# The first part of a convolution kernel with its TensorE work in blocks twice as long

## The chip, the cores and the metric

The kernel runs on one core of one Trainium2 chip. The metric is the device time of that core in microseconds (us). TensorE is called PE here, VectorE DVE, ScalarE ACT, GpSimd POOL, and SyncE SP, as in the profile.

## What is computed

The input x is 32 images of 128 channels of 64 x 64 pixels. The reference normalizes it in groups of four channels, and then convolves it through butterfly transforms along both image axes:

```python
def _kop2d(x, weight, kd1, kd2, k11, k12, k21, k22):
    x_f = tensor_product(xc, _c(k11), _c(k12), False)      # complex 64x64 matrices along h and w
    w_f = tensor_product(wc, _c(kd1), _c(kd2), False) * math.sqrt(H * W)
    prod = jnp.einsum('bihw,oihw->bohw', x_f, w_f)
    out = tensor_product(prod, _c(k21), _c(k22), True)
    return jnp.real(out)
...
x = x + _L0_conv_ref(_gn(x), ...)
t = _to_tokens(x)
t = t + _L1_attn_ref(_ln_t(t), ...)
t = t + _L1_ffn_ref(_ln_t(t), ...)                         # 8 experts, the best 2 weighted
```

## The kernel before

The kernel has three parts that follow each other. The first transforms the images (`x_f`) and writes the result to DRAM as `xf`. The second mixes the channels at every frequency. The third transforms back and does the attention and the experts. The change is in the first part alone.

In the first part, an image b goes through three kinds of PE work, each in pieces. A piece fills one PSUM tile, which another engine then copies out.

- `pz` (`turn_over`, line 373): 8 transposes of 128 x 128 turn a quarter of the image. Four pieces, g = 0 to 3. ACT copies each piece out into the tile `z` with four copies (`turned`, L383; planner keys `zo`, two copies each).
- `pv` (`along_w`, L396): 32 matmuls on 64 x 64 tiles of the array, the transform along W. Eight pieces. ACT copies each out into `v` with one copy (`w_out`, L407; key `vo`).
- `pf` (`along_h`, L418): 8 matmuls of 128 x 128, the transform along H. Eight pieces. The copy into a tile `f` (`h_out`, L428; key `fo`) is on DVE, but for every fourth piece (f3 and f7), where it is on ACT. Two DMAs on SP then write it to `xf` (`store`).

A float32 matmul that is not a transpose has two records in the trace: 64 pv records belong to one pv piece, 16 pf records to one pf piece.

All PSUM tiles of this part come from one pool with the tag "ps", four tiles of 4 KB per partition. The images, the tiles z, v and f come from pools of 3, 2, 2 and 4 buffers.

The work is pipelined over images in steps s = 0 to 33: in step s, PE does the pz pieces of image s, the pv pieces of image s-1 and the pf pieces of image s-2. The loop at the end of the part adds these pieces to a planner (`Plan`), with an estimated duration, a due time (`at`, in steps), what it comes after, and what it takes and frees ("ps" has room for 4). The order of the PE pieces is fixed: `add` chains each PE operation to the one added before. On every other engine the planner runs, of the operations that are ready by its estimates, the one that is due first. The instructions are then written out in the order that it found, and each engine runs its own in that order.

The group normalization of an image is spread over the step before its pz pieces. DVE takes eight statistics of 512 pixels (`bn_stats`, L319) as the loads of x land, and one aggregate (L328). Then a small PE matmul averages over the groups (L332, tile `gps`, which comes from the pool "ps" too), DVE computes the spread (L337 to L339), a second small matmul averages that (L342), DVE adds a constant (L345, after which `gps` is free), POOL takes the power (`grstd`, L349), and DVE scales the image in four pieces (L362). `norm_on_pe(b, 0)` adds the operations up to the first small matmul, `norm_on_pe(b, 1)` those from the second on. In the first four images the scaling is on ACT instead.

In the loop of before, a step has four equal blocks of one pz piece, two pv pieces and two pf pieces. The two small matmuls of the next image's normalization stand around the pz and pv pieces of one of these blocks:

```python
            for g in range(4):
                at = s + 0.25 * g
                if g == min(s, 3) - 1:
                    norm_on_pe(s + 1, 0)
                piece("pz", s, g, at)
                for k in range(2):
                    piece("pv", s - 1, 2 * g + k, at + 0.04 + 0.04 * k)
                if g == min(s, 3) - 1:
                    norm_on_pe(s + 1, 1)
```

Between steps 12 and 16, POOL prepares the convolution's weights, eight transposes on PE (`pwr`, L298, again a tile from "ps") turn them, and DVE copies them out (`wst`, L303).

Of the kernel before, what the change touches and what calls it, by code (L numbers as in the profile page):

```python
# [90 lines left out]
def kernel(  # L91
# [28 lines left out]
    pf = dram.tile([n, n, P * n], F32, name="pf")  # L120
# [42 lines left out]
    with ExitStack() as ph1:  # L163
# [12 lines left out]
        def add(key, engine, us, at, run, after=(), take=(), free=(), late=0.0):  # L176
            after = [made[k] for k in after if k in made]
            if engine == "PE":
                after += on_pe[-1:]
            made[key] = plan.add(engine, us, SLOT * at, run, after, take, free, late)  # L180
            if engine == "PE":
                on_pe.append(made[key])
# [184 lines left out]
        def turn_over(b, g):  # L367
            def run():
                ps = tile_of["pz", b, g] = pp.tile([P, 2, 512], F32, tag="ps", name=f"pz{b}_{g}")
                pv = ps.rearrange("w u (k c) -> w (u k) c", c=P)  # L370
                for k in range(8):
                    h = 2 * (8 * g + k)
                    nc.tensor.transpose(pv[:, k, :], xs[b][:, h * n : (h + 2) * n], ident)  # L373
            return run

        def turned(b, g, r):

            def run():
                if g == 0 and r == 0:
                    zs[b] = zp.tile([P, n, n], F32, tag="z", name=f"z{b}")  # L380
                pv = tile_of["pz", b, g].rearrange("w u (k c) -> w (u k) c", c=P)
                for half in range(2):
                    nc.scalar.copy(  # L383
                        zs[b][half * n : (half + 1) * n, :, 32 * r + 8 * g : 32 * r + 8 * g + 8],
                        pv[r * n : (r + 1) * n, :, half * n : (half + 1) * n].rearrange("w h c -> w c h"),
                    )
            return run

        def along_w(b, g):
            def run():  # L390
                ps = tile_of["pv", b, g] = pp.tile([P, 2, 512], F32, tag="ps", name=f"pv{b}_{g}")
                for k in range(8):
                    for half in range(2):
                        rows = slice(half * n, (half + 1) * n)
                        for r in range(2):
                            nc.tensor.matmul(  # L396
                                ps[r * n : (r + 1) * n, half, k * n : (k + 1) * n],
                                zs[b][rows, 8 * g + k, :], pw[rows, r, :], start=True, stop=True,
                            )
            return run  # L400

        def w_out(b, g):

            def run():
                if g == 0:
                    vs[b] = vp.tile([P, n, P], F32, tag="v", name=f"v{b}")
                nc.scalar.copy(  # L407
                    vs[b].rearrange("h w (a c) -> h w a c", a=2)[:, :, :, 8 * g : 8 * g + 8],
                    tile_of.pop(("pv", b, g)).rearrange("h a (c w) -> h w a c", w=n),
                )  # L410
            return run

        def along_h(b, g):
            def run():
                ps = tile_of["pf", b, g] = pp.tile([P, 2, 512], F32, tag="ps", name=f"pf{b}_{g}")
                pl = ps.rearrange("c u m -> c (u m)")
                for j in range(8):
                    nc.tensor.matmul(  # L418
                        pl[:, j * P : (j + 1) * P], vs[b][:, 8 * g + j, :], ph.rearrange("h r m -> h (r m)"),
                        start=True, stop=True,  # L420
                    )
            return run

        def h_out(b, g):
            def run():
                f = tile_of["f", b, g] = fp.tile([P, 8, 2 * n], F32, tag="f", name=f"f{b}_{g}")
                copy = nc.scalar.copy if g % 4 == 3 else nc.vector.tensor_copy
                copy(f.rearrange("c w m -> c (w m)"), tile_of.pop(("pf", b, g)).rearrange("c u m -> c (u m)"))  # L428
            return run

        def store(b, g):
            def run():
                f = tile_of.pop(("f", b, g))

                for k in range(0, 8, 4):
                    nc.sync.dma_start(xf[b, :, 8 * g + k : 8 * g + k + 4, :], f[:, k : k + 4])
            return run
# [52 lines left out]
        def piece(kind, b, g, at):  # L490
            if not 0 <= b < B:
                return
            if kind == "pz":
                add(
                    ("pz", b, g), "PE", 1.0, at, turn_over(b, g), [("nm", b, k) for k in range(4)],
                    ("ps",), ("x",) if g == 3 else (),
                )
                for r in range(2):
                    add(
                        ("zo", b, g, r), "ACT", 1.2, at, turned(b, g, r),  # L500
                        [("pz", b, g)] + [("pv", b - 2, k) for k in range(8)] + ([("zo", b, 0, 0)] if g or r else []),
                        (), ("ps",) if r else (),
                    )
            elif kind == "pv":
                add(
                    ("pv", b, g), "PE", 1.12, at, along_w(b, g),
                    [("zo", b, k, r) for k in range(4) for r in range(2)] + ["wi"], ("ps",),
                )
                add(
                    ("vo", b, g), "ACT", 1.02, at, w_out(b, g),  # L510
                    [("pv", b, g)] + [("pf", b - 2, k) for k in range(8)] + ([("vo", b, 0)] if g else []), (), ("ps",),
                )
            else:
                add(("pf", b, g), "PE", 1.95, at, along_h(b, g), [("vo", b, k) for k in range(8)], ("ps",))
                on_act = g % 4 == 3
                add(("fo", b, g), "ACT" if on_act else "DVE", 1.02 if on_act else 1.22, at, h_out(b, g), [("pf", b, g)], ("f",), ("ps",))
                add(("fs", b, g), "SP", 0.9, at, store(b, g), [("fo", b, g)], (), ("f",), 5.0)
# [7 lines left out]
        for s in range(B + 2):  # L525
            if s == 0:
                norm(2)
            for g in range(4):
                at = s + 0.25 * g
                if g == min(s, 3) - 1:  # L530
                    norm_on_pe(s + 1, 0)
                piece("pz", s, g, at)
                for k in range(2):
                    piece("pv", s - 1, 2 * g + k, at + 0.04 + 0.04 * k)
                if g == min(s, 3) - 1:
                    norm_on_pe(s + 1, 1)
                for k in range(2):
                    piece("pf", s - 2, 2 * g + k, at + 0.12 + 0.07 * k)
                    if 4 <= s + 2 < B:
                        piece_of_image(s + 2, 2 * g + k)  # L540
            if 3 <= s + 2 < B:
                norm(s + 2)
            if s == 0:
                norm_on_pe(1, 0)
                norm_on_pe(1, 1)
            if s == 3:
                butterfly(0, "POOL", nc.gpsimd, 3.2, 4.5)
                add("sel", "POOL", 2.5, 99, select, [("nm", 4, 3)])
            if s == 6:
                add("wr", "PE", 0.6, 6.0, weight_rows, [("b0", 5), "sel"], ("ps",))  # L550
                add("wd", "DVE", 0.8, 6.0, weight_matrices, ["wr"], (), ("ps",))
                butterfly(2, "POOL", nc.gpsimd, 7.0, 4.5)
                add("wo", "DVE", 1.2, 9.0, output_matrices, [("b2", 5)])
                add("wm", "SP", 0.5, 10.0, weight_taps, [("b2", 5)], (), (), 4.0)
            if 20 <= s < 24:
                add(("ew", s), "SP", 1.0, s, expert_load(s - 20), [("pf", s - 3, 4)], (), (), 4.0)
            if 12 <= s < 16:
                k = s - 12
                add(("wr", k), "POOL", 5.0, s - 0.5, onto_rows(k), ["wm", ("pf", s - 3, 4)], ("f",))
                add(("wt", k), "PE", 1.1, s, rows_turned(k), [("wr", k)], ("ps",))  # L560
                add(("we", k), "DVE", 1.25, s, rows_out(k), [("wt", k)], (), ("ps", "f"))
# [4 lines left out]
    with ExitStack() as ph2:  # L566
# [146 lines left out]
        for w in range(n):  # L713
# [9 lines left out]
            for half in range(2):  # L723
                for t in range(4):
                    at = w + 0.5 * half + 0.125 * t
# [718 lines left out]
```

## Time and profile before

| | |
|---|---|
| time, median of 3 runs | 6058.34 us (6054.57 to 6061.50) |
| the profiled execution: span | 6062.4 us, 4.1 above the median |
| TensorE clock, mean | 0.991 |
| PE busy | 5891.6 us, 97% |
| DVE, ACT, POOL busy | 4221.2, 3756.5, 4191.0 us |
| first pz to last pf of the first part | 21.3 to 931.0 us |
| pf matmuls, first part | 491.2 us in 4096 records |
| pv weight loads and matmuls | 16384 records each |
| xf stores | 512 DMAs of 256 KB, 3.3 us from issue to landing |
| x loads | 256 DMAs of 256 KB, 4.5 us from issue to landing |

The span goes from the first to the last instruction of the one execution that was profiled; the execution's own time is not in the list of runs, so its span is set beside them. Times of single instructions come from that execution. A row of a timeline gives the start in us, the length in us, the engine, the line, the operation, the tiles that it writes and reads, the shape and the count of merged instructions; in brackets, the engine's idle time before it and what ended it. Matmuls overlap in the array, so the busy time of PE counts them until their modelled end.

### The profile page before, as it was taken

The page shows a single profiled execution, that of the slowest core. Times are in us where ns is not written, and L with a number is a line of the kernel's source. Part 1 is how long each engine was busy: PE and PEld are TensorE (multiplying, and loading weights), DVE is VectorE, ACT ScalarE, POOL GpSimd, SP SyncE. Part 2 cuts the span into 40 slices and gives each one's busy share as a digit, 9 for nine tenths or more (in the row PEclk, how much of TensorE's full clock was granted, in tenths as well). Part 3 has the DMA queues.
Part 4 walks back from the last instruction along what each step waited for, and adds up shares of the span by engine and source line. Part 5 has one row for each costly group of instructions (what it writes and reads, how often), then busy time and mean ns, then how long its engine had stood idle before and what let it go on. Part 6 is the DMA issues. An engine that isn't in the chain of part 4 may idle for free.

```text
span 6062.4 us, 219265 instructions
## 1 busy us (share of the span) xinstructions
PE 5891.6 (97%) x95372; PEld 4677.6 (77%) x95372; DVE 4221.2 (70%) x7696; ACT 3756.5 (62%) x7057; POOL 4191.0 (69%) x3765
## 2 busy tenths in 40 slices
PE   7999999999999999889999999999999999999998
PEld 7999999999999999776666666666666666666654
DVE  5565545555555555448878787787878878787878
ACT  7666664555555555366667667666766766676663
POOL 2110006666666666428898898989989898998988
PEclk9999999999999999999999999999999999999999
DMA  6767666666666666632313222231322223132100
GB/s 200 238 224 237 234 214 193 172 173 172 172 174 171 171 171 172 160 107 77 92 56 102 67 88 81 72 97 57 101 68 84 84 64 104 57 97 71 65 27 28
DMA packets 555044, 756.74 MB, mean 125 GB/s; under 512 B 58592, under 2 KB 319712, under 8 KB 549984
## 3 DMA queue, kind: packets, MB, share of 16 engines
q1 hardware_dynamic: 551856, 738.76, 41.0%
q8 instruction: 749, 12.27, 0.9%
q0 software_dynamic: 896, 2.62, 0.1%
q14 instruction: 215, 1.76, 0.1%
q10 hardware_dynamic: 1328, 1.32, 0.1%
HBM read 406.93 MB, written 335.54 MB: 122 GB/s over the span
## 4 chain that ended last, share of the span: by engine, by line
PE 88%; ACT 7%; issue 2%; DVE 1%; POOL 1%; DMA 1%; SPq 0%; ACTq 0%; POOLq 0%; DVEq 0%
PE pe L1296 28%; PE m L654 17%; PE g L632 9%; PE pf L418 7%; PE pu L877 6%; PE pp L1145 4%; PE py L899 4%; PE pg L1072 4%; PE pv L396 3%; PE px L1283 2%; ACT xn L1273 2%; ACT u L887 2%; PE pz L373 1%; PE pt L1021 1%; ACT z L383 1%
## 5 line engine op out<-in xcount | busy, mean ns | idle before, releaser
L1296 PE MATMUL pe<-ew_sb,xT 128*128 128x512 f32 x4096 | 1948.4, 597 | 18.6 <-DVE tm L1307 15.1
L1307 DVE TENSOR_TENSOR tm<-pe,oh 128x512 f32<-128x512 f32 x2028 | 1346.6, 684 | 478.9 <-PE pe L1296 456.6
L1332 POOL TENSOR_TENSOR tm<-tm 128x512 f32<-128x512 f32 x1014 | 1285.0, 1284 | 202.6 <-DVE tm L1307 199.3
L1296 PEld LDWEIGHTS pe<-ew_sb,xT 128*128 128x128 f32 x4096 | 701.6, 191 | 523.4 <-issue 400.1
L643 DVE COPY f<-g 128x1024 f32<-128x1024 f32 x508 | 622.3, 1225 | 644.4 <-PE g L632 644.2
L654 PE MATMUL m<-f,s 128*64 128x64 f32 x32768 | 1068.9, 224 | 1.1 <-ACT f L643 0.8
L654 PEld LDWEIGHTS m<-f,s 128*64 128x64 f32 x32768 | 999.0, 138 | 62.4 <-issue 1.5
L600 POOL COPY s<-l 128x512 f32<-128x512 f32 x512 | 547.2, 1105 | 526.4 <-issue 509.7
L643 ACT COPY f<-g 128x1024 f32<-128x1024 f32 x508 | 514.7, 1013 | 556.4 <-PE g L632 530.1
L1335 POOL TENSOR_TENSOR tk<-tk,tm 128x256 f32<-128x256 f32 x1014 | 753.9, 743 | 79.5
L1333 POOL TENSOR_TENSOR tm<-tm 128x512 f32<-128x512 f32 x507 | 650.3, 1283 | 39.8
L887 ACT COPY u<-pu 64x512 f32<-64x512 f32 x960 | 556.3, 579 | 135.1 <-PE pu L877 121.6
L632 PE MATMUL g<-c,wst 9*128 9x128 f32 x16256 | 599.6, 283 | 1.7 <-issue 1.5
L632 PEld LDWEIGHTS g<-c,wst 9*128 9x128 f32 x16256 | 503.0, 186 | 36.2 <-issue 1.5
L349 POOL TENSOR_TENSOR grstd<-gms,mhalf 128x1 f32<-128x1 f32 x32 | 17.8, 555 | 737.8 <-DVE gms L345 737.8
L1158 ACT ACTIVATE pp<-pp,m 128x128 f32<-128x128 f32 x1024 | 440.9, 431 | 124.2 <-PE pp L1145 99.2
L602 POOL TENSOR_SCALAR s<-l 128x512 f32<-128x512 f32 x256 | 511.3, 1997 | 0.0
L877 PEld LDWEIGHTS pu<-qw,r 128*128 128x128 f32 x3840 | 455.1, 193 | 62.8 <-ACT u L887 49.0
L877 PE MATMUL pu<-qw,r 128*128 128x128 f32 x3840 | 475.8, 277 | 25.1 <-ACT u L887 25.1
L1289 ACT COPY xT<-px 128x512 f32<-128x512 f32 x256 | 150.2, 587 | 563.2 <-PE px L1283 560.1
L418 PE MATMUL pf<-ph,v 128*128 128x128 f32 x4096 | 491.2, 278 | 6.2 <-issue 1.4
L418 PEld LDWEIGHTS pf<-ph,v 128*128 128x128 f32 x4096 | 467.0, 192 | 16.0 <-ACT z L383 7.1
(169 smaller groups left out, 8569.6 us busy)
## 6 DMA issues: line engine op xcount, KB each, us to landing
xf<-f SPq DMA_DIRECT2D x512, 256.0 KB, 3.3
pf<-o SPq DMA_DIRECT2D x1024, 128.0 KB, 3.3
l<-xf SPq DMA_DIRECT2D x1012, 128.0 KB, 3.2
r<-pf SPq DMA_DIRECT2D x504, 256.0 KB, 4.7
x<-in_x_dram SPq DMA_DIRECT2D x256, 256.0 KB, 4.5
y<-in_x_dram SPq DMA_DIRECT2D x32, 2048.0 KB, 9.3
out_dram<-so SPq DMA_DIRECT2D x256, 256.0 KB, 2.2
tw<-in_tw_dram SPq DMA_DIRECT2D x6, 384.0 KB, 7.5
```

The source lines that it names most:

```text
L418: nc.tensor.matmul(pl[:, j * P : (j + 1) * P], vs[b][:, 8 * g + j, :], ph.rearrange("h r m -> h (r m)"), start=True, stop=True,)
L600: nc.gpsimd.tensor_copy(dst, src)
L632: nc.tensor.matmul(pg[g // 2][:, g % 2, m * P : (m + 1) * P], wst[rows, 16 * half + 4 * t + m, :], c[rows].rearrange("r h k -> r (h k)"), ...
L643: copy(f.rearrange("i m (g o) -> i m g o", g=2), tile_of["g", w, half, t][k].rearrange("i g (o m) -> i m g o", o=4))
L654: nc.tensor.matmul(ps[hh * n : (hh + 1) * n, q, :], s[:, h].rearrange("i k b -> i (k b)")[:, B * r : B * r + n], f[:, h, r, :], start=(r = ...
L877: nc.tensor.matmul(ps[:, k, :], rs[b, e][:, k * P : (k + 1) * P], qw.rearrange("w r m -> w (r m)"), start=True, stop=True,)
L887: nc.scalar.copy(u[r * n : (r + 1) * n, :, oh * n + 8 * e : oh * n + 8 * e + 8], ps[oh * n : (oh + 1) * n, :, r * n : (r + 1) * n].rearran ...
L1296: nc.tensor.matmul(ps, tile_of["xT", b, i // 4][:, i % 4, :], ew_sb[:, es, :].rearrange("d e c -> d (e c)"), start=True, stop=True,)
L1307: nc.vector.tensor_tensor(tile_of["tm", b, i // 2][:, i % 2, es, :], tile_of.pop(("pe", b, i, half)).rearrange("p (e c) -> p e c", c=P), t ...
L1332: nc.gpsimd.tensor_tensor(tm[:, k, 0:4, :], tm[:, k, 0:4, :], tm[:, k, 4:8, :], ALU.add)
L1333: nc.gpsimd.tensor_tensor(tm[:, :, 0:2, :], tm[:, :, 0:2, :], tm[:, :, 2:4, :], ALU.add)
L1335: nc.gpsimd.tensor_tensor(t[:, lo : lo + 2, :], t[:, lo : lo + 2, :], tm[:, :, m, :], ALU.add)
```

## The change

The loop of a step runs over two blocks instead of four. A block holds two pz pieces, four pv pieces and four pf pieces. The due times are set to match. The two parts of `norm_on_pe` stand around the pz and pv pieces of the first block in steps 1 and 2 and of the second block from step 3 on.

```diff
-            for g in range(4):
+            for g in (0, 2):
                 at = s + 0.25 * g
-                if g == min(s, 3) - 1:
+                turn = g == (0 if s < 3 else 2) and s > 0
+                if turn:
                     norm_on_pe(s + 1, 0)
-                piece("pz", s, g, at)
                 for k in range(2):
-                    piece("pv", s - 1, 2 * g + k, at + 0.04 + 0.04 * k)
-                if g == min(s, 3) - 1:
+                    piece("pz", s, g + k, at + 0.04 * k)
+                for k in range(4):
+                    piece("pv", s - 1, 2 * g + k, at + 0.08 + 0.04 * k)
+                if turn:
                     norm_on_pe(s + 1, 1)
-                for k in range(2):
-                    piece("pf", s - 2, 2 * g + k, at + 0.12 + 0.07 * k)
+                for k in range(4):
+                    piece("pf", s - 2, 2 * g + k, at + 0.24 + 0.065 * k)
                     if 4 <= s + 2 < B:
                         piece_of_image(s + 2, 2 * g + k)
```

## The prediction

> **What bounds the kernel now.** I began with the busy time by stage, because a share over 6062 us hides the first part. From 200 to 880 us, the steady stretch of the first part:
>
> ```profile
> 200.00:880.00 680.00, 672.71 (x16536) 646.05 (x16528) 395.09 (x557) 462.76 (x638) 54.55 (x142) 1.00 0.68 229
> ```
>
> The columns are the window, its length, busy time of PE, PE's weight loads, DVE, ACT, POOL, then granted clock, DMA share, GB/s. PE is busy 672.7 of 680 us at full clock. ACT has 463 us, so it is no bound on average. What counts is whether it has a PSUM tile empty when PE wants it. The timeline of PE over one image shows the pattern (start, length, engine, line, tiles, matmul records):
>
> ```profile
> 507.64 1.04 PE L373 MATMUL pz<-ident,x 128*128 128x128 f32 x8
> 508.61 2.10 PE L396 MATMUL pv<-pw,z 64*64 64x64 f32 x128
> 510.63 3.84 PE L418 MATMUL pf<-ph,v 128*128 128x128 f32 x32
> 514.31 1.04 PE L373 MATMUL pz<-ident,x 128*128 128x128 f32 x8
> ...
> 520.98 0.28 PE L332 MATMUL gps<-gmv,gmean 128*128 128x1 f32 x2
> 521.12 1.07 PE L373 MATMUL pz<-ident,x 128*128 128x128 f32 x8
> 522.12 2.09 PE L396 MATMUL pv<-pw,z 64*64 64x64 f32 x128
> 524.14 0.38 PE L342 MATMUL gps<-gms,gmean 128*128 128x1 f32 x2
> 524.63 3.84 PE L418 MATMUL pf<-ph,v 128*128 128x128 f32 x32
> 528.31 1.04 PE L373 MATMUL pz<-ident,x 128*128 128x128 f32 x8
> ```
>
> A block (one pz piece, two pv, two pf) takes 514.31 - 507.64 = 6.67 us, and nothing waits in it. The block with the norm's two small matmuls takes 528.31 - 520.98 = 7.33. An image is 3 x 6.67 + 7.33 = 27.33 us. The ACT timeline of the same stretch:
>
> ```profile
> 507.89 1.01 ACT L428 COPY f<-pf 128x1024 f32<-128x1024 f32 x1 [1.53 <-issue]
> 508.80 2.35 ACT L383 COPY z<-pz 64x512 f32<-64x512 f32 x4
> 511.17 1.93 ACT L407 COPY v<-pv 128x1024 f32<-128x1024 f32 x2
> 515.38 2.36 ACT L383 COPY z<-pz 64x512 f32<-64x512 f32 x4 [2.28 <-PE pz L373]
> ```
>
> A pz tile needs four ACT copies, 511.17 - 508.80 = 2.37 us, 0.59 each, though PE fills it in 0.9. This is the slowest eviction here: a pv tile needs one copy (next start after about 0.92, end after 1.01). One pz per block leaves ACT over 2 us idle in every second block.
>
> **The change, part by part.** The built program has the same instructions. PE's order becomes pz pz, pv x4, pf x4, twice per image. The norm's second matmul (g2) moves from behind pv5 to behind pv7, before pf4.
>
> *Removed: half of the turns between kinds.* Eight pz records at 0.109 us (x8 in 1.04 less the last one's 0.272, over 7), 32 groups of four pv records at 0.0585 (starts of single records) and 32 pf records at 0.1117 make 0.87 + 1.87 + 3.57 = 6.31. So 0.35 of the 6.67 lies in turns: about 0.14 pz to pv, 0.21 pv to pf, none pf to pz. By the merged rows instead of single starts it is 0.29. I take 0.35: two blocks less, so 0.70 us per image.
>
> *Added: waits for a PSUM tile.* The pool has four tiles "ps" for everything PE writes. I replay half an image, from the first pz's start as 0, with ACT to PE handover 0.05 (z ended at 51.21, the pv waiting for it began at 51.26). Every half now begins with the ACT copy of f7 or f3: it starts at 0.25 (507.89 - 507.64), the z copies at 1.16.
>
> First half, four tiles: pz0, pz1 end at 1.75; pv0, pv1 run from 1.89 to 3.76. pv2 takes pz0's tile, free at 1.16 + 2.37 = 3.53: no wait, ends 4.70. pv3 takes pz1's tile: free at 1.16 + 4.74 = 5.90, so it starts at 5.95, **1.25 late**, and ends at 6.89. pf0 needs pv0's tile, free at 5.90 + 1.01 + 0.05 = 6.96; the turn ends no sooner. Four pf at 1.79 and the turn's 0.21 give 14.25, against 13.33 for two blocks: **+0.92**.
>
> Second half: gps (taken before pz2, given back only after g2) holds a tile through all four pv, so three are left. pz2 ends at 1.01, its last record drains at 1.22, z copies run from 1.27 to 3.64 and 6.01. pz2, pz3 and pv4 (2.03 to 2.97) fill three tiles. pv5 waits for pz2's: 3.69, 0.72 late, to 4.63. pv6 waits for pz3's: 6.06, 1.43 late, to 7.00. pv7 waits for pv4's: 7.07, to 8.01. g2 and the turn: the block with the norm costs 7.33 - 6.67 = 0.66 more now. Of that, g1 is 0.14 (521.12 - 520.98). Two waits are in it too, from the list of who waited for whom in the same stretch (us, times, longest):
>
> ```profile
> PEld pf L418 <- ACT z L383: 5.2, 25, 0.6
> ...
> PEld pv L396 <- DVE gms L339: 4.0, 24, 0.2
> ```
>
> g2 waits 0.17 for DVE, which will have long been done behind pv7, and pf4 0.21 for pz2's tile, which will have been free for 4 us. Both go; g2 itself is the rest, 0.14. With it, the turn's 0.21 and 7.15 of pf the half ends at 15.51, against 6.67 + 7.33 = 14.00: **+1.51**.
>
> Sum 2.43 per image, 29.76 for 27.33. The saving is inside. Thirty of the 34 steps (2 to 31) hold all three kinds: 30 x 2.43 = 73.
>
> *Hidden work.* g2 later makes the norm later: gr, POOL's power (0.55) and four scalings (2.98) end some 4.2 us after g2, and f4, f5, f6 stand behind them on DVE (1.13 apart). f4's copy then ends near 13.5 of the half. The next pz0 wants its tile at 15.5, pv0 wants f6's near 17.4 and it is free at 15.8: about 2 us of cover, so I cost it at nothing. If the cover went, each us late would be a us on PE. Stores and loads on SP keep their order of kind, but come four tiles in a row: 2 MB in 7.2 us is 291 GB/s; each tile has about 13 us until it is needed again, landing takes 3.3. Nothing.
>
> *Smaller terms.* In steps 12 to 15 a pwr tile is taken behind pf7, and DVE's wst copy, which frees it, stands behind f4, f5 and two bn statistics. So the next first half too has three tiles: at least 0.9 each, at most 0.9 + 3.7 (longest wait of a gbs for an x load). I take 1.5 x 4 = 6, nearer to the first row. The steps outside the regular 27.33 (PE waiting for late x loads and the like) add some 9 us now; part of that falls into the new waits: -5, between 0 and -9. The last steps hold no pz and only save turns: -1. The ramp up to 62 us waits for the loads and ACT: 0, bounds -3 and +5.
>
> Sum: 73 + 6 - 5 - 1 = +73. The profiled execution's span is 6062.4 us, 4.1 above the median of the three runs; 6062.4 + 73 = 6135 there, 6131 as a median.
>
> [...] Would the new waits lower PE's clock? [...] Three windows of 3.41 us that each ended in a clock of 0.5 (columns as above; PE busy is 1.25 of 3.41, 0.40 of 3.41, 1.78 of 3.40):
>
> ```profile
> 45.94:49.35 3.41, 1.25 (x24) 0.94 (x16) 0.00 (x0) 3.41 (x4) 0.00 (x0) 1.00 0.01 2
> 28.87:32.28 3.41, 0.40 (x3) 0.35 (x3) 3.31 (x9) 3.33 (x7) 0.00 (x0) 1.00 1.00 304
> 2653.70:2657.10 3.40, 1.78 (x13) 1.35 (x12) 2.20 (x7) 3.17 (x10) 0.00 (x0) 1.00 0.47 130
> ```
>
> So a window 52% busy has lost the clock once; other windows of 45 to 53% kept it, and those at 60% or more, too (the drop at 936.8 us fell into matmuls of 9 rows, another kind of load). The new second half leaves PE idle for about 0.5 and 1.2 us (the waits less the 0.2 in which matmuls still drain), 0.9 apart: a window that holds both is 50% busy, and one in six images would place one so. A lowered stretch is at least 3.4 us at half speed, 1.7 us lost. That is 30/6 x 1.7 = 9 us at the lower end, and 30 x 1.7 = 51 if every image fell. I take nothing for the likeliest case. [...]
>
> **Rivals.**
>
> *PE's clock drops in the second halves.* For it: the row at 2653.7. Against it: the windows that kept the clock. +9 to +51 on top, 6140 to 6182; chance 0.13.
>
> *Eviction keeps up, and only the turns are saved.* If ACT emptied the pz tiles in time, each image would give 0.70 + 0.17 + 0.21 = 1.08, 32 x 1.08 = 35 us: 6024, faster. This is decided by the z copy alone: both halves wait 16 z copies less 6.0 us in sum; at 0.59 that is 3.4, it meets the 1.08 at 0.44 us per copy, and is gone at 0.38. The view of the z copies' line has 0.560 as the shortest of 512, so little speaks for it: 0.04. No change lies between, near 0.44: 0.02.
>
> *The burst of stores makes x late.* x statistics wait for loads now (91.6 us in 49 times, longest 3.7). They have about 2.4 us of room before gr and the scalings, then 2 us before f4 blocks pz0. Loads would have to be over 4 us later than PE needs; each further us costs up to 30: 6145 to 6190. Chance 0.05.
>
> *The waits are there, but smaller* (turns dearer than read, waits overlapping with irregular ones): +25 to +55, 6083 to 6113, chance 0.11.
>
> **How the numbers follow.** The likeliest, 0.65, is 6131 with its own range of 6113 to 6150 (2.43 +/- 0.4 per image is 12, the small terms 7). Reaching into the smaller waits below and the clock above, 8 in 10 lie in 6100 to 6167. About 0.2% (12 us) is what a measurement of this kernel can tell from no change. Faster 0.04, same 0.02, slower 0.94.
>
> **What would show it.** In the changed profile: an image every 29.8 us for 27.33; PE idle before pv, released by ACT z L383, some 1.2 us in the first half and 0.7 and 1.4 in the second; the z copies unchanged at 0.58 and in unbroken rows of eight; first part ending near 1004 for 931; the second and third part unchanged; the clock at 1.00 from 60 to 950 us. Wrong would be: PE rows without gaps before pv (then the tile count is wrong), PEclk below 9 tenths within the first part (the clock rival), waits of gbs on DMA in front of gr (the stores).

## The result: 2.9% slower, more than twice the predicted loss

The changed kernel takes 6235.87 us (median of 5 runs, 6231.82 to 6246.81), the kernel before 6061.50 beside it (5 runs, 6054.57 to 6064.81): a ratio of 1.0292, 95% interval 1.0279 to 1.0304. That is 174 us; forecast were 73, and the range ended at 6167. The sign was right, the size was not.

All of it lies in the first part. The last pf matmul starts at 1099.3 us of the profiled execution in place of 931.0 (+168.3); its span is 6233.0 us in place of 6062.4 (+170.6). The stretch from 200 to 880 us, with the same columns as in the prediction (busy time of PE, weight loads, DVE, ACT, POOL; clock; DMA):

```profile
200.00:880.00 680.00, 582.37 (x13759) 558.55 (x13749) 339.16 (x480) 384.82 (x534) 52.59 (x140) 0.98 0.57 194
```

PE is busy 582 us where it was 673, and the clock is no longer full (0.98 where it was 1.00). PE's timeline in a first half of an image shows what stands between:

```profile
570.65 1.91 PE L373 MATMUL pz<-ident,x 128*128 128x128 f32 x16
572.49 3.03 PE L396 MATMUL pv<-pw,z 64*64 64x64 f32 x192
576.59 1.08 PE L396 MATMUL pv<-pw,z 64*64 64x64 f32 x57 [1.07 <-ACT z L383]
578.14 0.34 PE L396 MATMUL pv<-pw,z 64*64 64x64 f32 x7 [0.47 <-issue]
578.41 9.04 PE L418 MATMUL pf<-ph,v 128*128 128x128 f32 x64
```

The first bracket is the forecast wait: three pv pieces (x192) run through, the fourth waits for pz1's tile, and ACT's eight z copies stand in one row, as the replay had them:

```profile
571.80 4.73 ACT L383 COPY z<-pz 64x512 f32<-64x512 f32 x8
```

The second bracket was not forecast. It lies 57 records into a piece of 64, where the code has no wait at all, and nothing released it ("issue"). I call such idle time inside a piece a stop. The list of waits of PE from 200 to 880 us (us in total, times, longest) has both kinds at nearly the same size:

```profile
PE pv L396 <- ACT z L383: 41.7, 48, 1.2
PE pv L396 <- issue: 36.8, 30, 3.4
PE pv L396 <- ACT f L428: 9.6, 9, 1.4
PE pf L418 <- issue: 7.8, 7, 1.8
```

And the four pf pieces after it took 9.04 us in place of 7.4, because the clock was halved for one window, right after one in which PE had been busy 1.86 of 3.40 us:

```profile
575.30:578.70 3.40, 1.86 (x82) 1.58 (x74) 0.71 (x2) 3.35 (x6) 0.00 (x0) 1.00 0.55 171
578.70:582.10 3.40, 3.40 (x18) 3.40 (x18) 0.11 (x1) 1.62 (x2) 0.00 (x0) 0.50 0.02 5
582.10:588.00 5.90, 5.90 (x55) 5.90 (x54) 4.49 (x7) 0.47 (x1) 0.00 (x0) 1.00 0.66 220
```

I added up the distances between the starts of all PE records from 62 us to the last pf, by kind, in both traces. A record's usual distance is "work"; what goes beyond it is sorted by where it lies.

| us | before | after | change | forecast |
|---|---|---|---|---|
| work | 811.2 | 812.9 | +2 | 0 |
| turns between kinds, g2 and its waits | 52.3 | 21.7 | -31 | -34 |
| waits between pieces or at a change of kind (tiles) | 6.5 | 94.8 | +88 | +104 |
| stops inside a piece (over 0.3 us) | 5.4 | 79.8 | +74 | none |
| lower clock | 0 | 25.1 | +25 | none |
| small rest | -6.3 | 2.9 | +9 | none |
| sum | 869.0 | 1037.3 | +168 | |

The forecast column is 0.70 and 0.38 us per image over some 31, and 3.47 us over 30 images. Tiles and turns together came to +58. The stops inside pieces and the clock are what the prediction lacks.

### The profile page after: what moved, and what is told of

It reads as the page before. It is cut to its first block, busy times and chain, and to the rows that moved or that the text cites. A ratio compares the mean times of both kernels' runs of the same rounds, so it can differ in the third digit from the quotient of the medians.

```text
span 6233.0 us, 219264 instructions
## 1 busy us (share of the span) xinstructions
PE 5924.0 (95%) x95372; PEld 4709.6 (76%) x95372; DVE 4254.5 (68%) x7696; ACT 3753.3 (60%) x7057; POOL 4188.1 (67%) x3765
## 4 chain that ended last, share of the span: by engine, by line
PE 84%; ACT 9%; issue 4%; DVE 1%; POOL 1%; DMA 1%; SPq 0%; ACTq 0%; POOLq 0%; DVEq 0%
PE pe L1298 27%; PE m L656 16%; PE g L634 9%; PE pf L418 6%; PE pu L879 5%; PE pp L1147 4%; PE py L901 4%; PE pg L1074 4%; ACT z L383 4%; PE pv L396 3%; PE px L1285 2%; ACT xn L1275 2%; ACT u L889 1%; PE pt L1023 1%; PE po L1344 1%
## 5 line engine op out<-in xcount | busy, mean ns | idle before, releaser
L418 PEld LDWEIGHTS pf<-ph,v 128*128 128x128 f32 x4096 | 479.8, 198 | 12.7 <-issue 9.9
```

Of the source, the lines that this page charges most:

```text
L418: nc.tensor.matmul(pl[:, j * P : (j + 1) * P], vs[b][:, 8 * g + j, :], ph.rearrange("h r m -> h (r m)"), start=True, stop=True,)
```

## What the stops are

The page has a DMA queue of instructions, q8. In the kernel before and in the kernel after it moved 749 transfers of 16 KB (the line is from the page of before):

```profile
q8 instruction: 749, 12.27, 0.9%
```

The run with fewer instructions, told of below, has 28,672 PE records less (162,072 for 190,744) and 637 transfers, 112 less: 256 records each, exactly.

```profile
q8 instruction: 637, 10.44, 0.7%
```

At 256 each, the 749 transfers are 191,744 instructions. The trace of before has 190,744 PE records and 1,056 of PE's sequencer, 191,800 in all. So I take q8 to be PE's queue.

A pv piece is 64 matmul and 64 weight-load records, 128 instructions in 0.94 us, or 137 per us; a pf piece is 32 in 1.79 us. I set the records of q8 beside the stops. I take a transfer as landed when its record ends. In the changed kernel there are 48 stops of over 0.3 us inside pv pieces, and every one ends 1.14 to 1.58 us after an instruction transfer has landed (median 1.36). In the first part two transfers never start closer than 3.27 us (5% are under 3.36). At that distance PE gets 256 instructions in 3.3 us, 78 per us, against 137 in pv. With runs of two pv pieces, 256 instructions, the stops inside pv pieces were 4 us in the kernel before; with runs of four, 512, they are 69 us in the changed kernel.

The place of the stops says the same more sharply. Counted from the start of the program over all PE instructions of the trace (matmuls, weight loads and those of PE's sequencer), every one of the 56 stops of over 0.3 us in the changed kernel, pf pieces included, comes after 192 or 193 instructions beyond a multiple of 256. So do all stops in the eight other kernels here that have any. Inside a piece PE stopped at one place of the 256 alone; I take it to be where one transfer's instructions end and the next one's begin.

Many stops appear from a run of 384 instructions on: 83 us in the run with three pv pieces in a row, told of below. How many instructions PE holds ahead no run shows directly.

The kernel before had such stops already, and I did not read them. Its timeline of PE from 205 to 245 us, from a stretch that I had counted among "late x loads and the like":

```profile
207.63 1.83 PE L418 MATMUL pf<-ph,v 128*128 128x128 f32 x14
210.53 2.27 PE L418 MATMUL pf<-ph,v 128*128 128x128 f32 x18 [1.07 <-issue]
```

A stop 14 records into a piece of 16, with nothing to wait for. Seven such stops, 5 us in all, lie in the part, and all end 1.13 to 1.46 us after an instruction transfer's landing.

## The experiments

Two theories: TILES (the forecast waits for PSUM tiles, and the lower clock that follows them) and FETCH (the supply of PE's instructions limits a run of four pv pieces). But for the last one, each experiment is one execution, with another of the kernel before beside it or with several. The executions of the kernel before lie between 6054.57 and 6074.09 us.

**Fewer instructions for the same columns.**

```diff
-                for k in range(8):
...
-                            nc.tensor.matmul(
-                                ps[r * n : (r + 1) * n, half, k * n : (k + 1) * n],
-                                zs[b][rows, 8 * g + k, :], pw[rows, r, :], start=True, stop=True,
-                            )
...
+                        nc.tensor.matmul(
+                            ps[r * n : (r + 1) * n, half, :], pw[rows, r, :],
+                            zs[b][rows, 8 * g : 8 * g + 8, :].rearrange("p c h -> p (c h)"), start=True, stop=True,
+                        )
```

> The changed kernel, but a pv piece is 4 matmuls that stream 512 columns of z against fixed weights pw, in place of 32 that stream 64 columns: the same columns through the same quarters of the array, 16 records in place of 128. (h and w of a piece come out exchanged, so the transform is another one; sizes and order are the same.) Theory FETCH (PE's instruction transfers of 16 KB, 256 instructions each, do not keep up in a run of four pv pieces, 512 instructions): the stops inside pv pieces, 69 us in the changed kernel's first part, go below 10; waits for PSUM tiles stay; 6130 to 6175 us. Theory TILES (all of the loss is waiting for PSUM tiles and the lower clock that follows): no change, 6220 to 6250.

Measured: 6152.98 us. The stops inside pieces are gone; the list of waits of PE from 200 to 880 us has only tiles (a third row, 1.3 us, is for the tile of the weights' transposes):

```profile
PE pv L395 <- ACT z L383: 65.9, 64, 1.3
PE pv L395 <- ACT f L427: 9.7, 9, 1.4
...
```

And the timeline is the replay of the prediction, start by start:

```profile
569.64 0.28 PE L332 MATMUL gps<-gmv,gmean 128*128 128x1 f32 x2
...
573.29 1.09 PE L395 MATMUL pv<-z,pw 64*64 64x512 f32 x8 [0.55 <-ACT z L383]
575.67 2.13 PE L395 MATMUL pv<-z,pw 64*64 64x512 f32 x16 [1.29 <-ACT z L383]
...
585.20 1.91 PE L373 MATMUL pz<-ident,x 128*128 128x128 f32 x16
...
591.14 1.09 PE L395 MATMUL pv<-z,pw 64*64 64x512 f32 x8 [1.29 <-ACT z L383]
```

In the second half pv5 starts 3.65 us and pv6 6.03 us after the half's first row, where the replay had 3.69 and 6.06; in the first half pv3 starts at 5.94 for 5.95. A regular image takes 29.79 us; 29.76 were forecast. Part of that closeness is luck: in the first half pf starts 0.12 us sooner than in the replay and takes 0.10 us longer.

**The same exchange before the change.**

> The same exchange of roles in pv in the kernel before, as the base for the run above: its stops inside pv pieces are 4 us, so both theories expect 6045 to 6070 us, unless a matmul of 512 columns has another price than eight of 64, which is then read here.

Measured: 6053.41 us, 26.9 us per image. That is 13 us below the 6066.52 beside it, and in the profile the part ends at 910.9 us for 931.0. Between the two runs with the exchange lie 100 us, not the 73 of the forecast. The exchange makes the image of before 0.44 us shorter and leaves the one after at the length of the replay, which ACT's z copies set (13 us over 30 images), and five stretches of lower clock, 17.1 us, are among it.

**The control: the exchange with the old count.**

```diff
-zs[b][rows, 8 * g + k, :], pw[rows, r, :], start=True, stop=True,
+pw[rows, r, :], zs[b][rows, 8 * g + k, :], start=True, stop=True,
```

> The control for the exchange of roles: the changed kernel with pw as the fixed weights and z streamed, but in 32 matmuls of 64 columns a piece as in the changed kernel, so 128 records again (h and w of a piece come out exchanged). Theory FETCH: the count of instructions decides, so the stops inside pv pieces come back, 50 to 90 us, and the time with them: 6205 to 6265 us. Theory ROLE (the stops come from loading z as weights, not from the count): as the run with 512 columns, 6140 to 6170.

Measured: 6243.41 us, with 74 us of stops in 52 places inside pv pieces, ending 1.21 to 1.65 us after a landing. The count decides, not which operand is held. Its waits of PE:

```profile
PE pv L396 <- issue: 41.1, 31, 3.9
PE pv L396 <- ACT z L383: 41.0, 47, 1.2
```

**The change in two halves.** First the pairs of pz alone:

```diff
+                for h in range(2):
+                    for k in range(2 * h, 2 * h + 2):
+                        piece("pv", s - 1, 2 * g + k, at + 0.08 + 0.04 * k + 0.16 * h)
+                    if turn and h == 0:
+                        norm_on_pe(s + 1, 1)
+                    for k in range(2 * h, 2 * h + 2):
+                        piece("pf", s - 2, 2 * g + k, at + 0.16 + 0.065 * k + 0.05 * h)
...
```

> Half of the change: two pz pieces in a row, but then pv pv pf pf pv pv pf pf, with the second small matmul of the norm behind the first two pv. FETCH: a run of two pv pieces is 256 instructions, as before the change, so stops inside pieces stay below 10 us in the part; what is left are tile waits in front of pf1 (0.2 us) and, while gps is held, pv5 and pf4 (0.7 and 1.0): about 28.7 us per image, 6085 to 6125. If pairs of pz alone made the stops inside pv: above 6160.

Measured: 6121.75 us, within FETCH's range, mostly 29.1 us per image, stops inside pv pieces of 1.9 us in all. The clock fell all the same, in seven stretches of 3.4 us. Two windows in a row (columns as above) show one of them, after a window in which PE was 59% busy:

```profile
401.30:404.70 3.40, 2.02 (x85) 1.73 (x77) 0.90 (x3) 3.30 (x7) 0.74 (x2) 1.00 0.93 304
404.70:408.10 3.40, 3.40 (x18) 3.40 (x17) 3.40 (x4) 1.59 (x2) 3.34 (x8) 0.50 0.18 64
```

Then the runs of four alone:

```diff
+                piece("pz", s, g, at)
                 if turn:
                     norm_on_pe(s + 1, 1)
                 for k in range(4):
...
+                    if k == 2:
+                        piece("pz", s, g + 1, at + 0.2)
+                        for j in range(4):
+                            piece("pv", s - 1, 2 * g + j, at + 0.23 + 0.035 * j)
+                    piece("pf", s - 2, 2 * g + k, at + 0.05 + 0.065 * k + (0.17 if k > 1 else 0))
...
```

> The other half: pv in runs of four, but the two pz pieces apart (pz, pf pf, pz, pv x4, pf pf), the norm's small matmuls around the first pz. TILES: pv3 wants pz1's tile at 3.8 us after pz1's start and has it at 3.5, so no wait, and two turns per image are saved: 26.6 us per image, 6030 to 6050. FETCH: four pv pieces are 512 instructions in 3.7 us, and transfers of 256 start no closer than 3.3 us, so PE stops 1 to 2.5 us per run, all inside pv pieces: 29 to 32 us per image, 6105 to 6200 with the clock's drops.

Measured: 6213.75 us, above both ranges but of FETCH's kind: 57 stops inside pv pieces, 119 us, and 85 us at the lower clock in the part. From 200 to 880 us PE waits for a tile in two places, 2.6 us in all, and it stops all the same, here after 217 of 256 records:

```profile
513.59 1.04 PE L373 MATMUL pz<-ident,x 128*128 128x128 f32 x8
514.56 3.42 PE L396 MATMUL pv<-pw,z 64*64 64x64 f32 x217
519.38 0.81 PE L396 MATMUL pv<-pw,z 64*64 64x64 f32 x39 [1.41 <-issue]
```

The two halves of the change cost 56 and 148 us against the kernel before beside them (6065.34), the whole 174: they overlap.

**A step in between.**

> A step in between: three blocks a step, with 3, 3 and 2 pv pieces in a row (and as many pf; 1, 1 and 2 pz), the norm's small matmuls around the pz piece of the middle block. FETCH: a run of 384 instructions is more than one transfer of 256 and less than two, so the stops fall between the two pieces' 4 us and the four pieces' 120: 10 to 50 us, all in the third piece. One turn less per image saves 0.35; the pair of pz waits about 0.7 for a tile: 6065 to 6115 us. If the stops were a matter of time in pv or of tile waits and not of the count: under 10 us of stops.

Measured: 6196.5 us, above the range: 83 us of stops in 37 places, nearly all in the third piece. Another 27 us are the second small matmul waiting for DVE, which I had not counted either. The direction held and the size did not. The law that I had in mind, in proportion to the count beyond 256, is wrong: one stop took 2.2 us on average here and 2.1 in the run of four before, whether a run goes 128 or 256 instructions beyond.

**Taking the tile waits away.** Half of the z copies go to DVE.

```diff
-                    nc.scalar.copy(
+                    copy = nc.vector.tensor_copy if r else nc.scalar.copy
+                    copy(
...
-                        ("zo", b, g, r), "ACT", 1.2, at, turned(b, g, r),
+                        ("zo", b, g, r), "DVE" if r else "ACT", 1.2, at, turned(b, g, r),
```

> The changed kernel with half of each pz piece's copies (r = 1) on DVE in place of ACT, so that a pz tile is free after two copies on each engine, about 1.2 us in place of 2.37. TILES: the waits of pv for z (about 90 us) shrink below 25 and nothing else stops PE: 6035 to 6075 us. FETCH: the same waits shrink, but the stops inside pv pieces stay at 60 to 100 us, now from the second piece of a run on: 6100 to 6140.

Measured: 6264.10 us, above both ranges and slower than the change itself. Waits of pv for z fell (41.7 us in the changed kernel, 27.3 here, from 200 to 880 us), and the stops inside pieces rose from 69 to 107 us; the time at the lower clock in the part rose from 55 to 82 us. The list of waits from 200 to 880 us:

```profile
PE pv L397 <- issue: 55.5, 35, 3.1
PE pv L397 <- DVE z L384: 23.3, 41, 3.1
...
PE pv L397 <- ACT z L384: 4.0, 4, 1.0
```

I read this so: waiting for a tile had been time in which instructions arrived. Why the stops grew by more (38 us) than all waits between pieces and before pv shrank (from 89 to 65 us) stays open.

> Both edits: half of the z copies on DVE and pv with 16 records a piece (h and w exchanged as above). Both theories: no stops inside pieces, few waits for tiles, and the saved turns of 0.35 us show: 6020 to 6055 us. More than 6075 would mean a third cause.

Measured: 6073.51 us, 27.2 us per image, but 31.2 in the four steps with pwr: above the range, and just below where a third cause was to be looked for. PE still waits for tiles, some 35 us from 200 to 880 us. Against 26.9 before the change with the same exchange, the longer blocks still gain nothing.

**The tile of gps.** Behind the first pv of four, in place of the last:

```diff
 for k in range(4):
     piece("pv", s - 1, 2 * g + k, ...)
+    if turn and k == 0:
+        norm_on_pe(s + 1, 1)
```

> The run with 4 matmuls of 512 columns per pv piece (h and w of a piece exchanged), and the norm's second small matmul behind the first of the four pv pieces, so that gps gives its tile back about 4 us sooner. By the replay pv5 then takes the tile of gps near 3.4 us, pv6 that of pz2 without a wait, and only pv7 waits for pz3's at 6.06: 7.0 in place of 8.0 us at the end of pv, less some 0.2 for one more turn: 29.0 to 29.2 us per image for 29.8, 6120 to 6140 us for 6153. If the tile of gps did not matter (the replay right by chance): 29.8 again.

Measured: 6104.98 us and 28.55 us per image, below the range: the tile matters, by 1.24 us per image where I expected 0.7.

> The changed kernel with the same move of the norm's second small matmul, and pv as it was (128 records a piece). FETCH: a wait for a tile is time in which instructions still arrive, so what the tile gives back comes again as stops inside pieces: 6215 to 6250 us, against 6236. If the two losses simply add: 20 us less, 6205 to 6222.

Measured: 6226.83 us, 9 less than the changed kernel, where the run without stops gained 48. Stops inside pv rose from 69 to 107 us. That speaks for FETCH; with one run, and ranges that overlap up to 6222, it is weak evidence by itself.

**A version that might beat both.** The second small matmul directly behind pz, in the kernel before:

```diff
                 piece("pz", s, g, at)
+                if turn:
+                    norm_on_pe(s + 1, 1)
                 for k in range(2):
                     piece("pv", s - 1, 2 * g + k, at + 0.04 + 0.04 * k)
-                if g == min(s, 3) - 1:
-                    norm_on_pe(s + 1, 1)
```

> The kernel before with one edit: the norm's second small matmul stands directly behind the pz piece in place of behind the two pv pieces, so that gps gives its tile back before pv and pf want tiles, and DVE's three small operations run beside pz. In the kernel before the block with the norm costs 0.66 us more than the others; in the run with the pz pieces apart the same two matmuls stood around pz and cost 0.15 and 0.18. If that holds: 0.33 us less in each of 29 images, about 10 us: 6046 to 6057 against 6061. If DVE is late for the second matmul (an f copy of 1.2 us in its way), no change.

Measured: 6066.53 against 6067.02 us (11 and 15 executions), a ratio of 0.9998 (0.9989 to 1.0008): no difference. The image does take 27.0 us in the regular steps, and the part ends 5 us sooner in the profile (925.9), but a stop of the same kind came back in the pf pieces:

```profile
521.04 0.94 PE L418 MATMUL pf<-ph,v 128*128 128x128 f32 x6
523.84 3.06 PE L418 MATMUL pf<-ph,v 128*128 128x128 f32 x26 [1.86 <-issue]
```

That one, too, ends 1.27 us after a landing. Why the 5 us do not show in the time stays open; in this profile the rest of the program takes 9 us longer than in that of before. No version run here that computes the same transform is faster than the kernel before. The exchange, which computes another one, may be: its one execution is 13 us below the one beside it, where the executions of the kernel before lie up to 20 us apart.

## Why the prediction was wrong, and where it was right

*Turns* (-34 forecast, -31 measured): right in size. The 0.35 us per block was there. Of the two waits around the norm only one was: from the start of g2 to pf4 it takes 0.49 us before and 0.245 after, which is the wait for pz2's tile. g2 itself starts 0.148 us after the last pv record in both kernels, just as a pf does in the kernel before, so PE lost nothing to DVE there.

*Waits for a PSUM tile* (3.47 us per image, 104 us): the mechanism was right, and in the run without stops the waiting pv pieces start within 0.04 us of the replay. In the changed kernel it shows as 88 us, because part of the waiting coincides with stops. In the half below, a stop of 1.75 us in the third pv piece takes the place of the wait for pz1's tile:

```profile
634.48 1.91 PE L373 MATMUL pz<-ident,x 128*128 128x128 f32 x16
636.32 2.77 PE L396 MATMUL pv<-pw,z 64*64 64x64 f32 x170
640.85 1.50 PE L396 MATMUL pv<-pw,z 64*64 64x64 f32 x86 [1.75 <-issue]
```

*"The built program has the same instructions"*: this is the step that failed. It priced instructions by their time in the array and the change of order by the turns and tiles, and took the supply of instructions for given. Nothing in the sum asked how many a run of four pv pieces needs per microsecond. The measured term is 74 us, and the control and the run with 512 columns show it to be the count. The lower clock adds to it. None of the rivals was this one.

*"Steps outside the regular 27.33 (PE waiting for late x loads and the like)"*: a wrong reading of the same thing. The rows that read "issue" in the middle of a piece were the sign of it, and I put the pv rows with "issue" down to turns.

*The clock* (nothing taken, 9 to 51 us as a rival): 25 us. The rival's range was right, and to take nothing was wrong. I counted windows from the tile waits alone. In the run without stops, where these act alone, five images lose the clock, about one in six, as the rival's lower end had it. With the stops, fifteen stretches of the part, 54.6 us, run at half clock. The window above lost it at 55% busy, where the row of before had 52%. In that window PE's gaps were 1.07 and 0.47 us.

*Smaller terms.* The four steps with pwr were to cost 1.5 us more each. In the run without stops they take 2.9 us more than a regular image, and 1.0 with the same exchange before the change: about 2.0 more each.

*Hidden work* (the late norm, the stores in fours, x loads): nothing of it appears among the waits of PE from 200 to 880 us, as said. *Eviction keeps up* and *the burst of stores*: not seen.

## What to carry to other kernels

Count instructions per microsecond before making a run of small matmuls longer: here 256 in a row passed almost without a stop and 384 did not. A piece like pf between two such runs takes 32 instructions in 1.79 us, 18 per us, where transfers of 256 every 3.3 us bring 78; that the supply catches up there is an estimate from these rates. An idle row that ends in "issue" inside a loop without waits deserves the question which transfer landed just before. And where two limits stand in the same place, taking one away shows the other: remove both in turn, and both together, before saying what either costs.

## What the runs showed of the hardware

- PE's instructions arrive in transfers of 256, in the first part of the changed kernel never closer than 3.27 us. In each of the nine kernels here that have stops, they stand at one place of the 256, and end on the median 1.24 to 1.42 us after a landing.
- Four matmuls of 512 columns make a row of 1.09 us, 32 of 64 through the same quarters of the array one of 1.16 us, and the exchange shortened an image from 27.33 to 26.9 us, with fixed weights pw and an eighth of the instructions.
- PE's clock fell to a half after a window of 3.4 us that was 55% busy, with single gaps of no more than 1.07 us, and after one that was 59% busy. Other windows of the changed kernel that were 54 or 55% busy kept it.
